# Layer 1's attention scores of seven images as 49 half-width products

## The chip, the cores and the metric

The kernel runs on one core of a Trainium2 chip. The metric is the device time of one execution in microseconds (us). Three runs of the kernel before gave 2888.49, 2889.4 and 2889.59 us; the median is 2889.4 us. PE is the matrix engine, PEld its weight loads, DVE, ACT and POOL are the three elementwise engines, SP only issues transfers. Each engine takes its own list of instructions and meets the others at semaphores.

## The reference

Input x has 8 images of 512 channels and 32 x 32 positions (1024 tokens), all float32. Two attention blocks run one after the other on every image:

```
layer 0:  h = groupnorm(x);  q, k, v = W h + b;  8 heads of 64 channels
          x = x + Wp softmax(q k / 8) v + bp
layer 1:  h = groupnorm(x);  one head of 512 channels
          x = x + Wp softmax((Wq h)(Wk h) / sqrt(512)) (Wv h) + bp
```

In layer 1 the kernel folds weights together: with g = (Wq, Wk product) h the scores are S = h^T g, a 1024 x 1024 matrix contracted over 512 channels, and z = (Wv, Wp product) h replaces the value and the output projection. The change touches how S is made, for seven of the eight images.

## The kernel before

**Products in seven parts.** Nearly every dense product is done by a Strassen-like scheme: both operands are cut in halves along both directions, sums of quarters are formed (`left_sums`, `right_sums`), and seven products p = 1 to 7 of the quarters replace eight. `wino` runs the seven in the order 1, (6, 2, 5, 7) or (2, 5, 6, 7), 4, 3. Partial sums stay in PSUM in three pools of banks called a, b and c with two buffers each. p = 1 goes to bank a and is copied out, 2 is added on top of it in a; 6, 7, 4 accumulate in bank b and are evicted after each; 5 and 3 accumulate in c. The last two steps of each scheme are put on a list, `tail`, and `finish()` emits them after the first step of the next scheme, so that the matrix engine has work while the last sums are evicted.

**Divided twice.** The products with the weights q, k and m (m gives g) are divided twice in `conv2` (L414): each of the seven outer products is itself done as seven inner products j of 128 x 128 x 256. Inner products of two outer products are done together as a `pair`; one pair holds product 7 alone, and there POOL adds finished blocks to each other (`more`, L444). An inner scheme has the steps 1, 6, 2, 5, 7 and, one scheme later, 3 and 4. Step 1 fills bank a and ACT copies it into bank b; 6, 7 and 4 accumulate in b, 2 in a, 5 and 3 in c. So step 7 on PE needs the eviction of step 6 to be over, step 4 that of step 7, and step 3 that of step 5. The quarter sums of the image (`inner_factors`, L411) are made by POOL, four instructions a factor.

**Scores of layer 1.** `layer1_scores` makes g with `conv2` and the list `gsteps` of eight sums of g's quarters. `scores1` (L625) then runs two schemes of the single division, each with 28 products of 128 x 128 x 512. DVE or ACT evicts each block of scores, ACT takes the exponential in place (L645, L648), and DVE sums the exponentials over rows (L654, L656) and forms the eight quarter sums of the exponentials in halves of 512 columns (L170 to L173). `layer1_rest` calls it, then makes z (`by_token`), then the values (`values1`).

**Background work.** Sums that are due later are put on the list `background`, and each step of a scheme takes one to four of them (`run_background`). The row statistics of the next image's group norm (`stats`, L98, L103) run so, inside the scores; its mean and its scale follow inside the scores and inside z as hooks.

**Order.** PE's instructions keep the order of the program. The instructions of DVE, ACT and POOL are put in order when the program is built, unless they are pinned, and each engine then executes its list in that order. One iteration of the loop over images works on layer 0 of image b and layer 1 of image b-1: attention0, projection, g, scores, z, values, then v, k and q of image b+1. Layer 1 of the last image stands alone after the loop and uses a single division for g as well.

## Time and profile before

| what | us |
|---|---|
| median of three runs | 2889.4 |
| time of the profiled execution | 2888.66 |
| its span, first to last instruction | 2886.8 |
| from one image to the next (start of the scores, 493.3 and 846.5) | 353.2 |
| a window of the scores of one image, 493.30 to 541.90 | 48.60 |
| in it: PE, DVE, ACT, POOL busy | 48.60, 31.41, 13.79, 1.04 |

The page lists busy times by engine, the chain of work that ended last and the costliest groups of instructions. Every float32 matmul of the program appears as two records[...], and every weight load likewise; a count "x256" is 128 matmuls. The time between two numbers of a matmul group is not its cost: matmuls overlap, and what counts is the distance from one start to the next.

### The profile page before, as it was taken

Reading aid. Unit: us, or ns where it says so; the run is one execution under the profiler, and the core shown is the slowest. Engines: PE = TensorE matmul, PEld = TensorE weight load, DVE = VectorE, ACT = ScalarE, POOL = GpSimd, SP = SyncE. Lnnn points to the kernel's source line nnn. Section 1 sums busy time; section 2 is a strip of 40 time slices with the busy share of each in tenths; the row PEclk is TensorE's granted clock in tenths of the full one; section 3 lists DMA queues with packets and bytes.
Section 4 is the critical chain, followed back from the end, with each engine's and each line's share of the span. In section 5 each row is a group of like instructions: output and inputs, shape, how many; then the busy total and the mean of one; then the engine's idle time right before and its main releaser. Section 6 shows DMA issues by size and latency. Waiting matters only on the chain.

```text
span 2886.8 us, 30280 instructions
## 1 busy us (share of the span) xinstructions
PE 2871.6 (99%) x11132; PEld 1555.1 (54%) x11132; DVE 2001.5 (69%) x2753; ACT 922.8 (32%) x1201; POOL 704.2 (24%) x781
## 2 busy tenths in 40 slices
PE   9999999999999999999999999999999999999998
PEld 5435635565355653557435574356833558345544
DVE  5587787667876578665786657876588665887554
ACT  1351452215522055211642116421163212632110
POOL 2113224032140321413223222323114131140000
PEclk9999999999999999999999999999999999999999
DMA  8722403123032221322212231122411224021201
GB/s 279 239 96 103 159 19 142 64 105 126 23 135 92 96 107 49 110 92 105 102 48 106 92 136 71 48 106 100 155 49 47 103 106 153 16 81 69 95 0 67
DMA packets 91586, 280.91 MB, mean 97 GB/s; under 512 B 10595, under 2 KB 36387, under 8 KB 82470
## 3 DMA queue, kind: packets, MB, share of 16 engines
q1 hardware_dynamic: 89638, 276.61, 26.4%
q10 hardware_dynamic: 1792, 2.29, 0.3%
q8 instruction: 90, 1.47, 0.2%
q14 instruction: 66, 0.54, 0.1%
HBM read 225.93 MB, written 52.93 MB: 97 GB/s over the span
## 4 chain that ended last, share of the span: by engine, by line
PE 98%; issue 1%; DVE 1%; DMA 0%; POOL 0%; SPq 0%; ACT 0%; DVEq 0%; POOLq 0%
PE sc L67 16%; PE av L67 16%; PE psb_sc L67 6%; PE psb_av L67 6%; PE psa_av L67 4%; PE psa_sc L67 4%; PE psc_av L67 4%; PE psc_sc L67 4%; PE psb_z L67 3%; PE psb_p L67 3%; PE psb_v L67 3%; PE psb_k L67 3%; PE psb_g L67 2%; PE psb_q L67 2%; PE psa_p L67 2%; PE psa_z L67 2%
## 5 line engine op out<-in xcount | busy, mean ns | idle before, releaser
L598 DVE TENSOR_TENSOR sum<-sum,e 128x1024 f32<-128x1024 f32 x384 | 519.3, 1352 | 41.8 <-DVE sum L598 1.4
L594 ACT ACTIVATE e<-sc 128x1024 f32<-128x1024 f32 x512 | 476.8, 1051 | 71.9 <-PE sc L67 71.9
L67 PE MATMUL sc<-q,k 64*128 64x512 f32 x2048 | 458.3, 596 | 0.0
L67 PE MATMUL av<-e,v 128*64 128x512 f32 x2048 | 453.6, 595 | 0.0
L67 PEld LDWEIGHTS sc<-q,k 64*128 64x128 f32 x2048 | 193.2, 186 | 238.4 <-ACT e L594 105.3
L67 PEld LDWEIGHTS av<-e,v 128*64 128x64 f32 x2048 | 141.4, 137 | 304.3 <-issue 302.3
L561 POOL TENSOR_TENSOR all_recs<-all_recs,rc 128x256 f32<-128x256 f32 x72 | 63.6, 884 | 611.2 <-DVE rc L559 603.6
L617 POOL TENSOR_TENSOR a<-a,r 128x512 f32<-128x512 f32 x56 | 114.2, 2039 | 264.4 <-DMA r<-rows 254.8
L559 DVE RECIPROCAL rc<-sums 128x256 f32<-128x256 f32 x72 | 126.5, 1757 | 47.7 <-PE sums L67 26.9
L612 ACT COPY a<-av 128x512 f32<-128x512 f32 x64 | 37.5, 586 | 305.4 <-PE av L67 305.4
L596 DVE TENSOR_TENSOR sum<-e,e 128x1024 f32<-128x1024 f32 x64 | 78.7, 1230 | 59.0 <-ACT e L594 58.9
L67 PE MATMUL psa_sc<-g,h 128*128 128x512 f32 x256 | 115.2, 595 | 0.0
L648 ACT ACTIVATE e<-e 128x512 f32<-128x512 f32 x96 | 59.7, 629 | 168.5 <-DVE e L647 168.5
L67 PE MATMUL psa_av<-e,z 128*128 128x512 f32 x256 | 113.3, 595 | 0.0
L128 POOL TENSOR_TENSOR rstd<-ve,mhalf 128x4 f32<-128x4 f32 x16 | 36.2, 2263 | 260.9 <-DVE ve L126 260.9
L140 ACT ACTIVATE h<-h,b,s 128x1024 f32<-128x1024 f32 x62 | 78.5, 1267 | 58.4 <-DMA h<-in_x 45.9
L411 POOL TENSOR_TENSOR inner_h<-h,inner_h 128x256 f32<-128x256 f32 x112 | 96.0, 860 | 2.7
L411 POOL TENSOR_TENSOR inner_h<-h 128x256 f32<-128x256 f32 x56 | 57.2, 1022 | 151.3 <-PE psc_av L67 151.3
L444 POOL TENSOR_TENSOR k<-k,k 128x256 f32<-128x256 f32 x28 | 20.1, 728 | 299.9 <-DVE u_k L439 299.9
L67 PEld LDWEIGHTS psa_sc<-g,h 128*128 128x128 f32 x256 | 48.1, 190 | 60.2 <-issue 54.5
L67 PEld LDWEIGHTS psa_av<-e,z 128*128 128x128 f32 x256 | 48.0, 190 | 57.3 <-issue 55.7
L652 POOL COPY sum<-e 128x1024 f32<-128x1024 f32 x8 | 8.8, 1102 | 283.5 <-ACT e L648 283.5
(327 smaller groups left out, 4992.1 us busy)
## 6 DMA issues: line engine op xcount, KB each, us to landing
x<-in_x SPq DMA_DIRECT2D x36, 512.0 KB
h<-in_x SPq DMA_DIRECT2D x32, 512.0 KB
spill<-x SPq DMA_DIRECT2D x32, 512.0 KB
h<-spill SPq DMA_DIRECT2D x32, 512.0 KB
x<-spill SPq DMA_DIRECT2D x32, 512.0 KB
out<-x SPq DMA_DIRECT2D x64, 256.0 KB
w_p<-sums_p SPq DMA_DIRECT2D x8, 1792.0 KB
r<-rows SPq DMA_DIRECT2D x112, 128.0 KB
```

The lines of the kernel that those rows point to most:

```text
L67: tc.keep_in_program_order(nc.tensor.matmul(*args, **kw))
L128: nc.gpsimd.tensor_tensor(rstd, ve, mhalf, ALU.pow)
L140: tc.keep_in_program_order(nc.scalar.activation(dst, src, AF.Identity, bias=b, scale=s))
L411: pin(nc.gpsimd.tensor_tensor(dst, x, y, ALU.subtract))
L559: nc.vector.reciprocal(rc, sums)
L561: nc.gpsimd.tensor_tensor(all_recs, all_recs, rc, ALU.add)
L594: nc.scalar.activation(e, sc, AF.Exp, scale=(C // 8) ** -0.5)
L596: nc.vector.tensor_add(total, es[0], e)
L598: nc.vector.tensor_add(total, total, e)
L612: nc.scalar.copy(dst, av)
L617: nc.gpsimd.tensor_tensor(dst, dst, r, ALU.mult)
L648: nc.scalar.activation(dst, dst, AF.Exp, scale=scale)
```

## The change

`scores1` stays for the last image only. The other seven use the new `scores1_twice`: each of the seven outer products p of the scores is divided again into seven inner products, 49 products with a width of 256, and each is two matmuls of 128 x 128 x 256. The inner scheme of `conv2` is taken out into `inner_steps`, which both use. POOL forms the inner factors of g (`query_factors`, four instructions for each p), at the start of the scheme before the one that uses them. The outer products come in the order 1, 2, 5, 6, 7, 3, 4. For outer products 1 and 5 ACT evicts four of the inner steps; elsewhere DVE adds each eviction to a block that is already there. For product 7 POOL adds blocks to each other, eight times, each 128 x 512. Exponentials are taken over tiles of 128 x 1024, row sums and quarter sums of the exponentials likewise; four of the eight quarter sums go to POOL. The last steps of g are now emitted after the first step of the scores. Four of the twelve statistics run inside g, the other eight in the scores; the hooks for mean and scale both move into z.

```
-                def step(j):
...
+        def inner_steps(uid, parity, k, mm, add, y, x, extra, after7, final, early=()):
+            def put(dst, n, at):
+                if x is None:
+                    (d,) = dst
+                    nc.scalar.copy(d, ps[n])
+                else:
+                    add(dst, ps[n], x(*at))
+            def step(j):
+                if j == 1:
+                    bank("a")
+                    mm(ps["a"], 1, True)
+                    bank("b")
+                    nc.scalar.copy(ps["b"], ps["a"])
...
+                elif j == 7:
+                    mm(ps["b"], 7, False)
+                    add(y(1, 1), ps["b"], [tmp["c5"]])
+                    extra(1, 1, False, True)
...
+                elif j == 4:
+                    mm(ps["b"], 4, False)
+                    put(y(1, 0), "b", (1, 0))
+                    extra(1, 0, True, True)
+                run_background(1)
+            step(1)
+            finish()
+            for g in early:
+                g()
+            for j in (6, 2, 5, 7):
+                step(j)
+            for g in after7:
+                g()
+            tail.extend([lambda: step(3), lambda: step(4)])
+            tail.extend(final)
...
+        def query_factors(f, uid):
+            t = big_tile(f"inner_{uid}", (P, 4, 2 * P))
...
+            for dst, x, y, op in (
+                (s1, a21, a22, ALU.add), (s2, s1, a11, ALU.subtract), (s3, a11, a21, ALU.subtract),
+                (s4, a12, s2, ALU.subtract),
+            ):
+                tc.keep_in_program_order(nc.gpsimd.tensor_tensor(dst, x, y, op))
...
+        def scores1_twice(b, f, gf, gsteps, first, uid, stats):
...
+            def add(dst, ps, x):
+                nc.vector.tensor_add(dst[0], ps, x[0])
+            def more(dst, x, y, r, cc):
+                nc.gpsimd.tensor_tensor(blocks(dst, r, cc)[0], blocks(x, r, cc)[0], blocks(y, r, cc)[0], ALU.add)
+            def exps(r, c):
+                for cc in (1, 0):
+                    nc.scalar.activation(e[c, cc, r], e[c, cc, r], AF.Exp, scale=scale)
+            def add_up(r, c):
+                if r == c:
+                    return [lambda: nc.vector.tensor_add(parts[r], e[c, 0, r], e[c, 1, r])]
+                return [
+                    *(lambda cc=cc: nc.vector.tensor_add(parts[r], parts[r], e[c, cc, r]) for cc in range(2)),
+                    lambda: nc.gpsimd.tensor_tensor(total[:, r, :], parts[r][:, 0, :], parts[r][:, 1, :], ALU.add),
+                ]
+            def product(s, p, y, x, before, small, after7=(), final=()):
+                def mm(ps, j, start):
+                    for i in range(2):
+                        matmul(
+                            ps[:, i, :], f[p][j][:, ts(i, P)], g2[p][j], start=start and i == 0, stop=True, skip_group_check=True
+                        )
+                def extra(r, cc, read, written):
+                    if p == 7:
+                        if read:
+                            more((0, 1), (0, 1), (1, 1), r, cc)
+                        if written:
+                            more((1, 1), (1, 0), (1, 1), r, cc)
...
+            product(0, 1, (1, 0), None, [2], gsteps[:2] + stats[:5])
+            product(1, 2, (0, 0), (1, 0), [5], gsteps[2:4], (), [lambda: exps(0, 0)])
+            product(2, 5, (1, 1), None, [6, 4], gsteps[4:] + stats[5:])
+            product(3, 6, (0, 1), (1, 0), [7, 3], add_up(0, 0))
+            product(4, 7, (1, 0), (0, 1), [], [])
+            product(5, 3, (0, 1), (0, 1), [], [], [lambda: exps(1, 1)], [lambda: exps(0, 1)])
+            product(
+                6, 4, (1, 0), (1, 0), [], add_up(1, 1) + add_up(0, 1), (),
+                [lambda: exps(1, 0), lambda: background.extend(add_up(1, 0) + steps)],
+            )
...
+            engines = [nc.vector] * 4 + [nc.gpsimd] * 4
...
-                gf = layer1_scores(b - 1, hf, inner)
+                gf, gsteps = layer1_scores(b - 1, hf, inner, [[], [lambda: background.extend(stats[:4])]])
+                _, _, mean, affine = norm_hooks(norm1, f"1_{b}")
...
-                hooks = [[], [], [lambda: background.extend(stats)]], [[], [], *means], affine
-                layer1_rest(b - 1, hf, gf, hooks, ahead)
+                layer1_rest(b - 1, hf, inner, gf, gsteps, stats[4:], [[], mean, [], affine], ahead)
```

## The prediction

> **What bounds the kernel now.** I read the shares by engine, then the chain, the groups by shape, single durations, and the time line around one image.

> ```profile
> PE 2871.6 (99%) x11132; PEld 1555.1 (54%) x11132; DVE 2001.5 (69%) x2753; ACT 922.8 (32%) x1201; POOL 704.2 (24%) x781
> PE 98%; issue 1%; DVE 1%; DMA 0%; POOL 0%; SPq 0%; ACT 0%; DVEq 0%; POOLq 0%
> ...
> 493.30:541.90 48.60, 48.60 (x124) 23.03 (x123) 31.41 (x56) 13.79 (x23) 1.04 (x1) 1.00 0.10 38
> ```

> PE holds 98% of the chain, and in the window of one image's scores (last line: length, then busy time of PE, PEld, DVE, ACT, POOL) it never rests. So a shorter PE list is worth its full length, and every new wait of PE costs its full length.

> ```profile
> L67 PE MATMUL psa_sc<-g,h 128*128 128x512 f32 x256 | 115.2, 595 | 0.0
> L67 PE MATMUL psb_g<-inner_h,w_m 128*128 128x256 f32 x294 | 75.1, 383 | 0.3
> ...
> 479.18 0.59 PE L67 MATMUL psa_g<-h,w_m 128*128 128x256 f32 x2
> 479.61 0.59 PE L67 MATMUL psa_g<-t_h,w_m 128*128 128x256 f32 x2
> ...
> 491.46 0.30 PEld L67 LDWEIGHTS psc_g<-h,w_m 128*128 128x128 f32 x2 [0.46 <-DVE c_g L439]
> ```

> The means 595 and 383 ns overlap. The starts say more: a pair of 256-wide records (one matmul) starts every 0.43 us, so 0.2165 a record; eight 512-wide ones run from 457.68 to 461.11, 0.429 each. The last line is g's stage, divided twice: PE waits for a DVE eviction there.

> ```profile
> L444 POOL TENSOR_TENSOR g<-g,g x28: 724/729/737, 485.4 to 2608.8; 128x256 f32<-128x256 f32 x28
> L617 POOL TENSOR_TENSOR a<-a,r x56: 1274/2156/2365, 150.8 to 2559.5; 128x512 f32<-128x512 f32 x56
> L306 POOL TENSOR_TENSOR prepare_q<-prepare_q 128x896 f32<-128x896 f32 x4 | 8.3, 2088 | 25.4 <-DMA x<-in_x 25.3
> L647 DVE TENSOR_TENSOR e<-psc_sc,u_sc 128x512 f32<-128x512 f32 x32 | 22.0, 686 | 8.4 <-PE psc_sc L67 8.4
> L654 DVE TENSOR_TENSOR sum<-sum,e 128x1024 f32<-128x1024 f32 x24 | 29.3, 1219 | 5.6 <-ACT e L648 5.6
> L856 DVE TENSOR_TENSOR x<-x,t_p x16: 673/1122/1246, 283.2 to 2589.4; 128x512 f32<-128x512 f32 x16
> L594 ACT ACTIVATE e<-sc 128x1024 f32<-128x1024 f32 x512 | 476.8, 1051 | 71.9 <-PE sc L67 71.9
> ```

> These are the prices: POOL adds (minimum, median, maximum where there are three), a DVE eviction, DVE sums, an exponential.

> [...] g's POOL adds keep to 724 to 737 ns beside DVE's evictions from PSUM, while L856, SBUF to SBUF beside POOL, has a median of 1122 ns and a minimum of 673. [...]

> **The change part by part, per image.** The instruction lists of the two built programs give the order on each engine, and no times. They are alike for all seven images.

> 1. PE's products. Before: 56 matmuls, 112 records x 0.429 = 48.05, and 0.28 of small waits inside (sum of the starts that come late). After: 98 matmuls, 196 x 0.2165 = 42.43. Gain 5.9 us, 41 us over seven images. A step is now two matmuls, 0.87 us, and the eviction of a step has one other step's time between (bank b: 7 after 6, 4 after 7; bank c: 3 after 5). An eviction starts 1.1 us after its step begins and takes 0.69; the next use comes at 2.6. So DVE may be 0.8 us late and no more.

> 2. Statistics in g: four of 0.67 us stand between g's evictions, the last just behind the first eviction of the pair that holds one product, where a step lasts 0.43. PE's step 7 there comes at 486.6 in place of 485.4, and one wait (491.46) goes away since the scores' first step lies between: +0.9.

> 3. Start of the scores (+1.0, from 0.6 to 1.45). ACT has the last four bias additions of g (0.72, later 0.65) before the copies of outer product 1; they wait for g's last evictions at about 495.2. Its eviction of step 5 ends near 499.9, PE's step 3 is due at 499.3. DVE's first two sums of g wait for the same bias, with POOL making factors beside them, so 0.65 to 1.1 each, and step 4 behind them is late.

> 4. Outer product 2 (+1.4, from 1.2 to 1.6). DVE: six evictions, 4.15, four sums of g, 2.6 to 4.4, and statistics left over, 1.7, in a scheme of 6.06 us of PE. The lists put a sum between evictions each time.

> 5. Outer products 5 and 6 (+0.4, from 0 to 0.85): row sums of 1.22, up to 2.1 beside POOL, ahead of evictions.

> 6. Outer product 7, then 3. POOL adds eight blocks of 128 x 512. From 256 (0.727) and 896 (2.083) elements a line gives 1.27; twice 0.727 bounds it at 1.45. DVE only evicts from PSUM then, so no contention. Count from U, the start of this scheme's step 6. The first add follows the eviction at U + 1.85, the chain of eight ends at U + 12.2 (POOL has finished its factors about 3 us before U), that is V + 6.1, where V = U + 6.06 is step 6 of outer product 3. PE itself does not need these. But the exponentials of the last blocks do: ACT takes the second at V + 6.2 to 7.3. **DVE's list has the row sum of exactly these exponentials ahead of the eviction of step 7**, although the program writes it a product later. So DVE waits to V + 7.3, sums to 8.55, evicts to 9.25; PE's step 4, due at V + 5.2, accumulates in that bank and starts at 9.3. Cost +4.2, with restart; to 5.3 if the adds take 1.45.

> 7. Free edits. Outer product 4 and z: DVE has 6.9 us of work in a scheme of 6.06, but z's first step (3.46 us of PE) follows; without that cover 0.9. The first POOL factors start as g's adds end (491.3 before, about 492.8 now), and are first needed at 495; POOL's later factors are a whole product ahead. ACT has about 17 us of work in 42. Quarter sums of the exponentials: POOL's four, 2.4 to 3.8 each, end well inside the values' 48 us. Mean and scale move later in z; rstd (2.26) and three small ones now queue behind two POOL subtractions, so the scale is ready near 567 where it was 555.9; ACT needs it at 575.4, since the image's load lands then. Without those 8 us it would delay the next image. SP has 512 rows in both programs; its loads after the scores wait for buffers that the scores have left by then.

> Sum: -5.9 + 0.9 + 1.0 + 1.4 + 0.4 + 4.2 = +2.0; a restarted PE loses about another 0.1 at each of several waits (104 ns late on the second record after 491.46), so +2.2. Times seven: +15 us. The profiled execution's 2888.66 becomes 2904; the median stands 0.7 above it, so 2905. All low ends together, -5.9 + 6.7 = +0.8, give 2895; all high ones, -5.9 + 10.9 = +5, give 2924.

> **The rivals.** (A) DVE's early row sum does not hold: the POOL chain ends before the eviction would start. For it: POOL is 76% idle in the profile. Against: eight adds need 10 us and the scheme has 6. Then -5.9 + 3.7 + 0.3 = -1.9, 2876. (B) The early waits (2 to 5) hide in one another, since a late PE gives DVE time, and only 6 stays: -5.9 + 4.3 = -1.6, 2878: faster. For it: the gaps of g's stage are small, 0.7 us an image. Against: g has no such sums in its schemes. All waits hidden would be 2848; the sign turns where the waits sum to 5.9. (C) POOL's adds meet contention and take 2.04 us as L617's mean does: the chain ends 6 us later, +8.2 an image, 2947. Against: L444's narrow spread. That PE's products do not shrink is excluded: g's stage shows their rate.

> **How the numbers follow.** The main case 0.72 (own range 2895 to 2924), B 0.12, A 0.06, C 0.04, a sum near zero 0.06. About 0.2% (5.8 us) is what a measurement can tell from none. Faster: A, B and a little, 0.19. Same: the middle and the low edge of the main case, 0.09. Slower 0.72. The range for 8 in 10 reaches down into B, to 2880, and up to 2924; A, the rest of B, C and the tails are left out.

> **What would show it.** Late starts of PE in outer product 3, at the last step 4 of bank b, of 4 to 5 us in each of seven images, with DVE idle ahead of a 128x1024 row sum, released by ACT, whose exponential was released by POOL. POOL's 128x512 adds at 1.27 to 1.45 us. Scores with 196 records at 0.2165 and, g's end to z's start, about 50.5 us in place of 48.6. PE waits of 0.5 to 1.5 us in outer products 1 and 2. Wrong if the POOL adds run near 0.7, if DVE's exponential is ready by V + 4, or if z or the values show new waits.

## The result and the profile after

The changed kernel takes 2906.48 us (median of five runs, 2902.85 to 2908.49) against 2888.85 us before (median of five runs, 2888.40 to 2889.59): a ratio of 1.006, with a 95% interval of 1.0045 to 1.0075. That is 17.6 us more. The forecast was 2905, slower, with a range from 2880 to 2924. The profiled execution took 2908.49 us, its span is 2906.6 (before: 2886.8).

The page of the changed kernel, shares by engine and then the chain that ended last:

```profile
PE 2852.4 (98%) x11720; PEld 1678.3 (58%) x11720; DVE 2098.9 (72%) x2760; ACT 953.8 (33%) x1222; POOL 1018.8 (35%) x1068
...
PE 90%; DVE 4%; POOL 3%; issue 1%; ACT 1%; DMA 0%; SPq 0%; DVEq 0%; POOLq 0%; ACTq 0%
```

PE has 588 records more, 84 an image, as counted. It is less busy, 2852.4 us for 2871.6. But its share of the chain has fallen from 98% to 90%; DVE and POOL have most of the difference. The window of one image's scores (length, then busy time and count of PE, PEld, DVE, ACT, POOL, then the granted clock of the matrix engine, DMA share, GB/s):

```profile
493.10:542.80 49.70, 45.28 (x198) 38.22 (x197) 35.15 (x56) 17.69 (x26) 33.34 (x37) 0.97 0.10 38
```

PE rests for 4.4 of 49.7 us, where it never rested. The mean clock that it was granted is 0.97 (1 is full speed), where it was 1.00; nothing in the prediction answers to that.

The waits of PE, from the view that lists them by the engine and line that ended them (us in total, times, longest):

```profile
PE psb L67 <- DVE e L712: 29.8, 21, 3.7
PE psb_g L67 <- DVE u_g L521: 6.3, 7, 0.9
PE psb_av L67 <- DVE w_av L238: 1.9, 4, 0.5
```

Seven of the 21 waits in the first line are the long one, 7 x 3.7 = 26 of 29.8 us. Two groups of the page's list by line answer to the prices, POOL's additions and the first row sum:

```profile
L715 POOL TENSOR_TENSOR e<-e,e 128x512 f32<-128x512 f32 x56 | 69.9, 1268 | 21.3 <-DVE u L712 19.7
L724 DVE TENSOR_TENSOR sum<-e,e 128x1024 f32<-128x1024 f32 x14 | 17.1, 1221 | 25.5 <-ACT e L719 25.5
```

POOL's additions take 1268 ns, 1.27 as worked out. The row sum L724 has 25.5 us of idle DVE time ahead of it, seven times 3.6, all ended by ACT's exponential. Here is that place in the first of the seven images, from the time lines of POOL, ACT, DVE and PE (start, length, what, idle time before and what ended it):

```profile
523.54 10.21 POOL L715 TENSOR_TENSOR e<-e,e 128x512 f32<-128x512 f32 x8 [2.80 <-DVE u L712]
...
533.79 1.06 ACT L719 ACTIVATE e<-e 128x1024 f32<-128x1024 f32 x1 [1.51 <-POOL e L715]
...
534.88 1.23 DVE L724 TENSOR_TENSOR sum<-e,e 128x1024 f32<-128x1024 f32 x1 [3.63 <-ACT e L719]
536.02 0.68 DVE L712 TENSOR_TENSOR e<-psb,c 128x512 f32<-128x512 f32 x1
...
532.01 1.03 PE L67 MATMUL psc<-inner,h 128*128 128x256 f32 x4
536.76 2.08 PE L67 MATMUL psb<-sg,inner_h 128*128 128x256 f32 x4 [3.72 <-DVE e L712]
538.62 1.76 PE L67 MATMUL psb<-inner,inner_h 128*128 128x256 f32 x4
540.23 1.03 PE L67 MATMUL psa<-g,t_h 128*128 128x256 f32 x4
```

Read from top to bottom this is the chain of the prediction: eight additions, exponential, row sum, the eviction of step 7 behind it, and only then PE's step 4. With V = 527.70 (step 6 of outer product 3) POOL ends at V + 6.05 (said: 6.1), the exponential at V + 7.15 (7.3), the eviction at V + 9.0 (9.25), and PE starts at V + 9.06 (9.3).

The last two lines hold what was not foreseen. From 538.62 to 540.23 four records take 1.61 us from start to start, where four took 0.86 before the wait. The window view splits that stretch (PE's busy time and count come after the length; the granted clock is the third number from the end):

```profile
532.80:536.70 3.90, 0.24 (x2) 0.00 (x0) 1.82 (x3) 1.54 (x2) 0.95 (x1) 1.00 0.00 0
536.70:540.10 3.40, 3.34 (x8) 2.72 (x9) 1.29 (x3) 1.56 (x2) 0.00 (x0) 0.50 0.00 0
540.10:543.50 3.40, 3.40 (x18) 3.00 (x17) 2.90 (x4) 0.55 (x1) 0.00 (x0) 1.00 0.02 5
```

PE is idle for most of 3.9 us; then come 3.4 us at a granted clock of 0.50, the half rate, with 8 records; then 1.00 and 18 records in the same time. In five images this costs 1.74 us (the sum of the starts that come late after the wait). In the two others it costs 3.04: there the granted clock stays at half for 6.83 us, and PE works through some 6.0 of them.

### The profile page after: what moved, and what is told of

It is laid out like the page before. It is cut to its first block, busy times and chain, and to the rows that moved or that the text cites. A ratio compares the mean times of both kernels' runs of the same rounds, so it can differ in the third digit from the quotient of the medians.

```text
span 2906.6 us, 32039 instructions
## 1 busy us (share of the span) xinstructions
PE 2852.4 (98%) x11720; PEld 1678.3 (58%) x11720; DVE 2098.9 (72%) x2760; ACT 953.8 (33%) x1222; POOL 1018.8 (35%) x1068
## 4 chain that ended last, share of the span: by engine, by line
PE 90%; DVE 4%; POOL 3%; issue 1%; ACT 1%; DMA 0%; SPq 0%; DVEq 0%; POOLq 0%; ACTq 0%
PE sc L67 16%; PE av L67 15%; PE psb_av L67 5%; PE psa_av L67 4%; PE psc_av L67 4%; PE psb L67 4%; PE psb_z L67 3%; PE psb_p L67 3%; PE psb_v L67 3%; PE psb_k L67 3%; PE psb_g L67 2%; PE psb_q L67 2%; POOL e L715 2%; PE psa_p L67 2%; PE psa_z L67 2%; PE psc_v L67 2%
## 5 line engine op out<-in xcount | busy, mean ns | idle before, releaser
L617 DVE TENSOR_TENSOR sum<-sum,e 128x1024 f32<-128x1024 f32 x384 | 519.3, 1352 | 41.8 <-DVE sum L617 1.8
L613 ACT ACTIVATE e<-sc 128x1024 f32<-128x1024 f32 x512 | 476.8, 1053 | 72.2 <-PE sc L67 72.2
L67 PE MATMUL sc<-q,k 64*128 64x512 f32 x2048 | 458.4, 597 | 0.0
L67 PE MATMUL av<-e,v 128*64 128x512 f32 x2048 | 453.6, 596 | 0.0
L67 PEld LDWEIGHTS sc<-q,k 64*128 64x128 f32 x2048 | 193.5, 186 | 238.1 <-ACT e L613 105.2
L67 PEld LDWEIGHTS av<-e,v 128*64 128x64 f32 x2048 | 141.4, 137 | 304.3 <-issue 302.3
L67 PE MATMUL psa_av<-e,z 128*128 128x512 f32 x256 | 113.3, 596 | 0.0
L67 PE MATMUL psb<-inner,inner_h 128*128 128x256 f32 x392 | 106.5, 397 | 0.0
L140 ACT ACTIVATE h<-h,b,s 128x1024 f32<-128x1024 f32 x62 | 78.3, 1268 | 80.4 <-DMA h<-in_x 64.9
L411 POOL TENSOR_TENSOR inner_h<-t_h 128x256 f32<-128x256 f32 x84 | 85.0, 1015 | 17.9 <-PE psc_av L67 15.4
L67 PEld LDWEIGHTS psb<-inner,inner_h 128*128 128x128 f32 x392 | 78.2, 200 | 11.5
L719 ACT ACTIVATE e<-e 128x1024 f32<-128x1024 f32 x56 | 58.4, 1055 | 77.4 <-POOL e L715 42.0
L67 PE MATMUL psb_g<-inner_h,w_m 128*128 128x256 f32 x294 | 75.2, 384 | 6.3 <-DVE u_g L521 6.3
L67 PEld LDWEIGHTS psa_av<-e,z 128*128 128x128 f32 x256 | 48.1, 190 | 57.2 <-issue 56.5
L715 POOL TENSOR_TENSOR e<-e,e 128x512 f32<-128x512 f32 x56 | 69.9, 1268 | 21.3 <-DVE u L712 19.7
```

The source lines that it names most:

```text
L67: tc.keep_in_program_order(nc.tensor.matmul(*args, **kw))
L140: tc.keep_in_program_order(nc.scalar.activation(dst, src, AF.Identity, bias=b, scale=s))
L411: pin(nc.gpsimd.tensor_tensor(dst, x, y, ALU.subtract))
L613: nc.scalar.activation(e, sc, AF.Exp, scale=(C // 8) ** -0.5)
L617: nc.vector.tensor_add(total, total, e)
L715: nc.gpsimd.tensor_tensor(blocks(dst, r, cc)[0], blocks(x, r, cc)[0], blocks(y, r, cc)[0], ALU.add)
```

## Experiments

Two questions stand behind the 17.6 us. Is it the place of one row sum in DVE's list that makes the wait, or is POOL's chain too long wherever the sum stands? And what is the half rate? Each run was measured beside the kernel before on the same chip, which took 2888.2 to 2888.4 us there; the changed kernel's 2906.5 is from the result above, where before took 0.4 to 0.6 us more.

### The row sum moved behind the evictions

```
-                nc.vector.tensor_add(dst[0], ps, x[0])
+                tc.keep_in_program_order(nc.vector.tensor_add(dst[0], ps, x[0]))
...
-                    return [lambda: nc.vector.tensor_add(parts[r], e[c, 0, r], e[c, 1, r])]
+                    return [lambda: tc.keep_in_program_order(nc.vector.tensor_add(parts[r], e[c, 0, r], e[c, 1, r]))]
```

> The changed kernel with one difference: VectorE takes the additions of the scores and the row sum of the second diagonal quarter in the order written, so that this sum stands behind the three evictions of outer product 3 and the first of outer product 4. All work is kept. Theory (the sum's place in VectorE's list makes the wait): the wait of 3.9 us at step 4 of outer product 3 goes, and with it the time after it in which matmuls start 0.42 us apart instead of 0.216 (about 2 us per image). But ScalarE's copy for outer product 4 stands behind the two exponentials that wait for GpSimd's additions, and would end some 1.5 to 1.9 us after step 6 of outer product 4 is due. If a wait that short brings no half rate: 3.9 + 2.2 - 1.7 = 4.4 us saved per image, 2906.5 - 7 x 4.4 = 2876 us (2870 to 2884). If it brings the half rate as well: 2906.5 - 7 x 2.2 = 2891 us. Rival (GpSimd's chain is late for TensorE by any way, and its wait only changes its place): within 5 us of 2906.

Measured: 2875.4 us (2875.17 to 2876.2), ratio to before 0.9954 (0.9937 to 0.9971). The sign of the whole change has turned, with the same work, by the order of DVE's list alone. The edit moves two row sums an image, each behind four evictions; the sum of the first diagonal quarter moves too, but no matmul waited behind that one in the changed kernel. The wait has gone from outer product 3, and the shorter one foretold for outer product 4 is there, in PE's time line:

```profile
531.64 1.03 PE L67 MATMUL psb<-sg,inner_h 128*128 128x256 f32 x4
534.17 1.13 PE L67 MATMUL psb<-inner,inner_h 128*128 128x256 f32 x4 [1.50 <-ACT psb L459]
```

The second row starts 1.66 us late, behind ACT's copy. The window after it:

```profile
534.20:537.60 3.40, 3.40 (x16) 3.01 (x17) 2.19 (x3) 1.84 (x2) 0.00 (x0) 1.00 0.02 5
```

The clock stays at 1.00, and in all seven images no matmul after the wait is slow. The rival (POOL's chain binds by any way) is refuted as far as the sum goes: POOL's eight additions take what they took (1269 ns on the mean, 1268 before the edit).

### The exponentials behind the copy as well

```
-            product(5, 3, (0, 1), (0, 1), [], [], [lambda: exps(1, 1)], [lambda: exps(0, 1)])
+            product(5, 3, (0, 1), (0, 1), [], [], (), [lambda: exps(1, 1), lambda: exps(0, 1)])
```

and, so that ACT keeps to it:

```
-                    nc.scalar.copy(ps["b"], ps["a"])
+                    tc.keep_in_program_order(nc.scalar.copy(ps["b"], ps["a"]))
...
-                    nc.scalar.activation(e[c, cc, r], e[c, cc, r], AF.Exp, scale=scale)
+                    tc.keep_in_program_order(nc.scalar.activation(e[c, cc, r], e[c, cc, r], AF.Exp, scale=scale))
```

> As the run before, and the two exponentials of the second diagonal quarter stand on ScalarE behind the copy that begins outer product 4. All work is kept. Theory: nothing that waits for GpSimd's additions stands ahead of an eviction or a copy any more, so both the wait and the half rate after it go: 3.9 + 2.2 = 6.1 us per image, 2906.5 - 7 x 6.1 = 2864 us (2859 to 2870), 25 us below the kernel before. Rival (the lateness is handed on to the sums and exponentials of the last quarter and from there to the reciprocals or to GpSimd's part of the normalization): a new wait of 1 to 3 us per image at outer product 4 or in z, 2871 to 2885 us.

Measured: 2864.88 us (2864.66 to 2865.6), ratio to before 0.9917 (0.9901 to 0.9934), 24 us below the kernel before and 42 below the change as made. No new wait took the place of the two. The waits of PE by this kernel's list:

```profile
PE psb_g L67 <- DVE u_g L521: 6.3, 7, 0.9
...
PE psb L67 <- DVE e L712: 3.7, 14, 0.3
```

The 29.8 us of the changed kernel have become 3.7. So the cause of the wait is settled: a sum and two exponentials that nothing was in a hurry for, ahead of an eviction and a copy that PE was waiting for.

### The idle time filled

This kernel adds work: eight matmuls an image into a tile that nothing reads, where PE would stand idle. Theory C is that the half rate is an answer to PE's idle time.

```
                 elif j == 4:
+                    fill()
                     mm(ps["b"], 4, False)
...
+            def fill():
+                ps = acc_tile(f"fill_{uid}")
+                for n in range(8):
+                    matmul(ps[:, : 2 * P], f[3][1][:, :P], g2[3][1], start=True, stop=True)
...
+                    fill if p == 3 else lambda: None,
```

> The changed kernel with eight additional 128x256 matmuls per image (3.5 us at the rate of the profile, into a PSUM tile that nothing reads) on TensorE just ahead of step 4 of outer product 3, where TensorE otherwise stands idle for 3.9 us. The wait itself, its cause and all other work are as in the changed kernel. Theory C [...]: the granted clock stays at 1 there, matmuls after the wait start 0.216 us apart, and 1.7 to 3.3 us per image are saved: 2906.5 - 7 x 2.2 = 2891 us (2883 to 2895). Rival D (the half rate comes from what runs beside those matmuls: the row sum, the exponentials, late evictions): it stays, and the time is 2906 us or a few us more.

Measured: 2892.04 us (2889.38 to 2893.42): 14.4 us less than the changed kernel, with 3.5 us more work an image and the same wait for the same eviction. Windows of the idle stretch, now filled, and of what follows:

```profile
531.20:534.90 3.70, 3.70 (x18) 2.92 (x16) 1.59 (x2) 1.54 (x2) 0.99 (x1) 1.00 0.00 0
535.00:538.40 3.40, 3.21 (x15) 2.85 (x16) 2.43 (x5) 2.11 (x2) 0.00 (x0) 1.00 0.02 5
```

The row sum, the exponentials and the late evictions run beside these matmuls as before, and the clock is 1.00 in all seven images. The half rate is an answer to the idle time. This run also shows the change with its wait and without the half rate: 2892.0 us against 2888.4 before, a ratio of 1.001.

Half as many matmuls leave a part of the idle time:

```
-                for n in range(8):
+                for n in range(4):
```

> As the run before with four additional matmuls instead of eight (1.7 us), so that some 2.2 us of idle time are left at the same place. [...] Theory C [...]: part of the half rate stays, between the time with eight and 2906. Rival D: 2906 us.

Measured, with four matmuls: 2899.7 us (2895.56 to 2902.99). This lies between, as Theory C had it if any idle time counts; the author's other guess, no half rate after so short a rest and a time within 2 us of the kernel with eight, is missed. PE's start is 2.16 us late in every image (2.00 us of rest in the trace), and the half rate follows in four of the seven, at 1.68 us each; the last section shows what sets these four apart. One image without and one with, the idle stretch of the first and what comes behind the wait in each:

```profile
533.40:535.40 2.00, 0.11 (x1) 0.00 (x0) 1.77 (x3) 0.68 (x2) 0.00 (x0) 1.00 0.00 0
535.40:538.80 3.40, 3.29 (x15) 2.93 (x16) 2.43 (x5) 2.11 (x2) 0.00 (x0) 1.00 0.00 0
...
890.30:892.30 2.00, 2.00 (x7) 1.55 (x6) 0.69 (x1) 0.95 (x2) 0.00 (x0) 0.50 0.00 0
```

### Undoing parts: the statistics

```
-                gf, gsteps = layer1_scores(b - 1, hf, inner, [[], [lambda: background.extend(stats[:4])]])
+                gf, gsteps = layer1_scores(b - 1, hf, inner, [[], [lambda: background.extend(stats[:0])]])
...
-            product(2, 5, (1, 1), None, [6, 4], gsteps[4:] + stats[5:])
+            product(2, 5, (1, 1), None, [6, 4], gsteps[4:] + stats[5:9])
...
-            product(4, 7, (1, 0), (0, 1), [], [])
+            product(4, 7, (1, 0), (0, 1), [], stats[9:])
...
-                layer1_rest(b - 1, hf, inner, gf, gsteps, stats[4:], [[], mean, [], affine], ahead)
+                layer1_rest(b - 1, hf, inner, gf, gsteps, stats, [[], mean, [], affine], ahead)
```

> The changed kernel with one part undone: the first four steps of the statistics, which the change moved into g, stand in the scores again (nine of the twelve in outer products 1 and 5 and their tails, the last three in outer product 7). All work is kept. Theory: the wait of 1.06 us that the trace of the changed kernel has in g, 0.53 us per image above the kernel before, goes, and outer products 1 and 2 wait as before: 2906.5 - 7 x 0.53 = 2902.8 us. Rival (the additions of VectorE are late by the sum of its work at the start of the scores, so that statistics moved there cost as much as in g): 2906.5 us, plus or minus 1.

Measured: 2911.96 us (2909.12 to 2914.65), worse than the theory and than its rival. By the late starts of PE in the first image the wait in g does go (1.26 to 0.41 us). But outer products 1 and 2 now cost 2.33 in place of 1.64, and outer product 6 has a new wait of 1.02, because a statistics step and the row sum stand together ahead of an eviction: 0.69 + 1.02 - 0.85 = +0.86, times seven 6.0, which is what the time shows (5.5). Of these two places g was the cheaper one for the four statistics.

To take them out of the dense parts altogether, the kernel of 2864.88 us was given four steps each behind the evictions of outer products 6, 7 and 3:

```
-            product(0, 1, (1, 0), None, [2], gsteps[:2] + stats[:5])
+            product(0, 1, (1, 0), None, [2], gsteps[:2])
...
-            product(2, 5, (1, 1), None, [6, 4], gsteps[4:] + stats[5:])
-            product(3, 6, (0, 1), (1, 0), [7, 3], add_up(0, 0))
-            product(4, 7, (1, 0), (0, 1), [], [])
+            product(2, 5, (1, 1), None, [6, 4], gsteps[4:])
+            product(3, 6, (0, 1), (1, 0), [7, 3], add_up(0, 0) + stats[:4])
+            product(4, 7, (1, 0), (0, 1), [], stats[4:8])
...
```

The last four follow in outer product 3 (`stats[8:]` in its call), and none are left in g.

> The run with the sum and the exponentials behind (2864.9 us), and the statistics moved out of g and out of outer products 1 and 2: four steps each in the background of outer products 6, 7 and 3, where VectorE has 0.2 to 1 us free between its evictions. All work is kept. Theory: g's wait (0.53 us above before) goes, and of the waits at the starts of outer products 1 and 2 (1.6 us per image) the part that statistics ahead of an eviction make, 0.4 to 0.8 us: 2864.9 - 7 x (0.53 + 0.6) = 2857 us (2853 to 2861). Rival (an eviction of outer products 6, 7 or 3 is late behind a statistics step of 0.6 us, and TensorE waits there instead): 2861 to 2868 us.

Measured: 2895.22 us (2889.8 to 2902.46), 30 us worse than without the move, far outside both. DVE's time line at outer product 6:

```profile
515.90 1.64 DVE L724 TENSOR_TENSOR sum<-e,e 128x1024 f32<-128x1024 f32 x1
518.76 0.69 DVE L712 TENSOR_TENSOR e<-psa,e 128x512 f32<-128x512 f32 x1 [1.22 <-PE psa L67]
```

The eviction at 518.76 reads a bank that PE had finished near 516, and yet it waited for PE. In the built program it waits for step 1 of outer product 7 (517.62 to 518.65 in PE's time line), which reads g's first tile: the statistics hold x's tiles longer, and the tile of the exponentials that this eviction writes first came into the buffer of that g tile. PE's steps 3 and 4 were late by 2.3 and 1.1 us, with the half rate after it in three images. One buffer more tests this:

```
-NBIG = 32
+NBIG = 33
```

> The run with the statistics moved to outer products 6, 7 and 3 (2895.2 us), with 33 instead of 32 buffers in the pool of 4 KB tiles. All work is kept. In the trace of that run the first addition of outer product 6 into the exponentials' tile starts 1.2 us after the row sum ahead of it has ended, when step 1 of outer product 7 has ended on TensorE, and TensorE's steps 3 and 4 of outer product 6 are late by 2.3 and 1.2 us, in three images at half rate after that. Theory B (the statistics hold their inputs' buffers longer, so that this tile comes into the buffer of g's first tile, which step 1 of outer product 7 still reads): with one buffer more the tile comes into another, the wait goes, and what remains is the run with sum and exponentials behind, less 0.85 us in g and plus 0.1 to 0.6 us at the start of the scores: 2860 us (2857 to 2864). Rival (the statistics steps of 0.6 us ahead of the evictions of outer product 6 are the cause): 2885 to 2896 us.

Measured: 2866.06 us (2862.64 to 2868.01), ratio to before 0.9923 (0.9909 to 0.9937). The buffer was the cause of the 29 us, and the rival, that the statistics steps themselves make the wait, is refuted: they stand where they stood. What the move was meant to gain is not there, so that the forecast of 2860 (2857 to 2864) is missed by a little: g is 0.85 us an image shorter, but PE's step 4 of outer product 1 starts 1.0 us late in place of 0.48 (a sum of g has moved ahead of the eviction that it needs), and outer product 6 has 0.9 us of new waits. It is equal to the kernel of 2864.88 within what can be told.

### Undoing parts: the quarter sums, and the wait in the values

The changed kernel's trace has a wait in the values in four of seven images, with the time lines of DVE and PE:

```profile
602.48 7.51 DVE L783 TENSOR_TENSOR o<-o,r 128x512 f32<-128x512 f32 x1
...
611.78 1.55 PE L67 MATMUL psb_av<-t,z 128*128 128x512 f32 x3 [0.47 <-DVE w_av L238]
```

The same multiplication has a median of 692 ns. It reads two tiles in SBUF, and POOL runs a closed row of additions of 0.72 us from SBUF for the next image meanwhile. The kernel before has such a row in the values too, and its longest multiplication takes 1.24 us. The first question is whether POOL's four quarter sums, which the change put ahead of that row, make the difference:

```
-            engines = [nc.vector] * 4 + [nc.gpsimd] * 4
+            engines = [nc.vector] * 8
```

> The changed kernel with one part undone: all eight sums of the exponentials' quarters in z are VectorE's, instead of four on VectorE and four on GpSimd. All work is kept. In the trace of the changed kernel the values hold a wait of 0.73 us in four of the seven images, beside a VectorE multiplication of 7.5 us (0.69 elsewhere), while GpSimd forms factors of the next image. Theory V (GpSimd's four sums of z push its work on the factors into the multiplications of the values): no such wait in any image, 2906.5 - 4 x 0.73 = 2903.6 us, unless VectorE's four more sums of 1.2 us delay the evictions of z. Rival W (the wait hangs on the phase of the two engines' streams in the values, which these sums don't set): it stays in some images, 2904 to 2908 us. In the run with filled idle time it came in one image of seven and in the run with the sum behind in none, with the sums where the change put them, which speaks for W.

Measured: 2923.84 us (2923.16 to 2924.83). The wait in question is left in one image, where a multiplication takes 8.0 us and PE's start behind it is 1.14 us late; so it does not need POOL's four sums, as rival W had it. But a larger wait, 2.2 us in six images and 1.7 in the last, stands at the start of the values and makes the time. DVE's and PE's time lines:

```profile
583.99 0.69 DVE L780 TENSOR_TENSOR o<-psa_av,r 128x512 f32<-128x512 f32 x1 [1.90 <-PE psa_av L67]
584.60 0.68 DVE L159 TENSOR_TENSOR sz<-z,z 128x512 f32<-128x512 f32 x1
...
585.43 1.95 PE L67 MATMUL psc_av<-t,sz 128*128 128x512 f32 x4 [1.48 <-DVE sz L159]
```

It is not the four sums themselves: DVE sits idle for 1.90 us. With the other list the order changed, and the scaling of the first blocks, which waits for PE, stands ahead of z's sums, for which PE waits. That is the row sum's case again. As the order changed with the edit, the run does not say why four images became one.

A direct test delays POOL's row of additions, in the kernel of 2866.06 us: a copy of one column of x on POOL stands ahead of them, and they are pinned behind it.

```
+                tc.keep_in_program_order(nc.gpsimd.tensor_copy(g, done_x[0][:, :1]))
             background.extend(steps)
```

> The run before, and GpSimd's 28 additions for the factors of the next image's h (0.72 us each, back to back through the middle of the values) start only when VectorE has made the last additions of the values: a copy of one column of x on GpSimd stands ahead of them and waits for it. All other work is kept. Theory W (VectorE's multiplication of two SBUF operands takes 7.5 us, and TensorE then waits 0.63 + 0.1 us, where it meets this stream): no image has the wait of 0.73 us in the values, against four of seven in the changed kernel and two to four in others; 0 to 3 us less than the run before. Rival (the stream is not the cause): the wait stays in some images. Against both: the factors may be late for k, 17 us later, which would cost 1 us or more per image there.

Measured: 2867.64 us (2866.27 to 2868.12), no such wait in any image; but the run before, without the copy, had none either in its trace, so this says nothing. The copy let the row start at 602.1, in the midst of the values and not after them. The same edit in the changed kernel, where four images had the wait:

> The changed kernel itself with the one edit of the run before: GpSimd's additions for the factors of the next image's h wait, by a copy of one column of x on GpSimd, until VectorE has made one of the later additions of the values (602 us in the trace of the run before, where the stream otherwise begins near 583). All other work is kept. Theory W (VectorE's multiplications of two SBUF operands stand still for 7.5 us where they meet GpSimd's stream): the multiplications behind the gate still meet it, those ahead of it do not, so that the wait of 0.73 us comes in fewer images than four, most likely in none: 2903 to 2907 us. Rival (the wait has another cause): four images again, 2906.5 us. The difference in time is at most 3 us; the trace decides, by the number of multiplications of 7.5 us.

Measured: 2902.97 us (2901.65 to 2904.72), 3.5 us less than the changed kernel. No multiplication is longer than 1.14 us and no image has the wait. Part of the 3.5 us is the half rate: this trace has none in one image and two windows of it in one, where the changed kernel's trace has two windows in two. So the time decides nothing here, but the trace does: the edit touches POOL's list alone, and DVE's keeps the order of the changed kernel.

That POOL's row is what the multiplication waits for shows in its end as well. The traces of this document hold eighteen multiplications of 7.5 to 8.0 us, and each of them ends 0.47 us after the start of the last addition of POOL's row; PE was late behind every one. Seventeen of the eighteen start 0.07 to 0.12 us before POOL's next addition. Of eighteen others that start so, fifteen took 0.69 to 0.71 us, and there POOL's next addition took 1.15 to 1.19 us in place of 0.72; three took some 1.35 us. So either engine can be the one that gives way. Which one, and so why it is none to four of seven images in kernels that differ elsewhere, stays open.

## Why the prediction was right, and where it was not

The time and the sign were met, 2905 said and 2906.5 measured, and the wait that the prediction rests on was right in place, chain and size. That the number was met all the same is luck: the balance behind it, in us per image from the starts of PE's records that come late, has wrong terms that made up for each other.

| step | said | measured |
|---|---|---|
| 1 products | -5.9 | -6.0 |
| 2 statistics in g | +0.9 | +0.53 |
| 3 start of the scores | +1.0 | +0.98 |
| 4 outer product 2 | +1.4 | +0.66 |
| 5 outer products 5 and 6 | +0.4 | 0 |
| 6 wait behind the row sum | +4.2 | +3.88 |
| restarts | +0.2 | in the terms |
| half rate after the wait | - | +1.74 in five images, +3.04 in two: 2.11 |
| 7 "free edits": z, values | 0 | +0.08; 0.42 (0.74 in four of seven) |
| sum | +2.2 | +2.7 |

2.66 x 7 = 18.6, against 19.8 between the spans; where the rest is was not traced. Steps 1 to 6 alone, at their measured sizes, sum to +0.05 us an image, which is no change. What makes the kernel slower is the half rate behind the wait, 2.11, and the wait in the values, 0.42; the prediction had about 0.1 for a restart and nothing in their place. The run with the idle time filled says the same with 2892.0 us, where the half rate is missing.

**Step 1** was right: 196 records of 0.216 us, 42.3 us. The 0.28 us of waits inside the old scores are part of the 6.0.

**Step 2** was too large. PE's step 7 in g came 0.85 us later than before, not 1.2; the wait that should go did go (0.32).

**Step 3** was right in place and size: the first late start stands behind ACT's copy, which waits behind the bias additions (0.33), the second behind DVE's two sums and a statistics step (0.47).

**Steps 4 and 5** were too large. Here DVE's sums of g took 0.68 to 0.90 us beside POOL, near the low end of the range of 0.65 to 1.1 that was taken, and the start that was late already gave DVE time. Outer products 5 and 6 had none. So rival B was right in part: steps 2 to 5 cost 2.2 us and not 3.7. With the 3.88 of step 6 that just cancels the gain of step 1, so that B's sign, faster, does not come out either.

**Step 6** was right to 0.3 us in each of its members, and the runs show its cause: with the sum moved, the sign turns. That DVE takes its list in order, on which the case rests, shows in the same lines: PE's step 7 for the late eviction ran from 530.28 to 531.31, DVE was free from 531.25 on, and yet the eviction started at 536.02, behind the sum. A and C are refuted by the lines of the result (DVE idle 3.63 us; additions of 1.27). The prediction looked at the order of DVE's list, which the program's text doesn't give.

**The term that failed** is "a restarted PE loses about another 0.1". That was read from waits of 0.5 us. After 3.9 us PE loses 2.11 us on the mean. The trace of the kernel before does not show such a loss: after PE's first matmul its longest rest is 0.80 us, and from 9.2 us of the span to the last matmul the granted clock is 1.00. So the 0.1 was carried from waits of 0.5 us to one of 4.2. With the measured 2.11 in place of the 0.2 for restarts the sum would have been +4.1, 2918 us, a worse forecast from a better reason, since steps 2, 4 and 5 were 1.5 us too large together.

**Step 7** had one miss, and it is one of the prediction's own signs of being wrong: the values show a new wait. The step looked at where POOL's work ends, and not at POOL's factors for the next image, which run beside the multiplications of the values. What L856 shows in the trace before, an addition of two SBUF tiles that took 1.12 to 1.25 us beside POOL's additions and 0.67 where POOL was idle, was used for row sums and the sums of g, and not for this multiplication, which has two SBUF operands beside a POOL row; 7.51 us for 0.69 (8.02 in one run) is what it comes to here. The rest of the step held: the row sums, z and the scale hid as said, but for 0.08 us.

**The range.** The ends of the prediction's sum, +0.8 and +5, do not follow from the ranges that its steps give; with the restarts those make about +1.2 and +4.4. The measured time lies inside either way.

## What to carry to other kernels

Before a shorter list of the bottleneck engine is worth anything, look in the built order of every other engine for an instruction that waits for a slow neighbour and stands ahead of one that the bottleneck needs; four of the ten runs here turned on such a place, and putting two row sums an image behind four evictions each was worth more than the change cost (31 us to 17.6). Price a wait of the matrix engine of 2 us or more with the half rate that may follow: a rest of 2.00 us had it in four of seven images, and the one of 3.72 in all seven, where it cost 2.11 us an image, 14.8 of the 17.6. And a moved reader moves buffers: look at what each first write into a pool's tile waits for.

## What the hardware showed that was not expected

```profile
530.38:533.79 3.41, 1.59 (x8) 1.06 (x6) 0.00 (x0) 1.90 (x3) 2.23 (x2) 1.00 0.00 0
533.79:537.21 3.42, 1.52 (x7) 1.37 (x8) 2.78 (x4) 1.42 (x2) 0.00 (x0) 1.00 0.00 0
537.21:540.62 3.41, 3.41 (x18) 3.00 (x17) 3.06 (x5) 1.17 (x2) 0.00 (x0) 1.00 0.02 5
...
2289.57:2292.98 3.41, 1.43 (x7) 0.93 (x5) 2.19 (x5) 0.57 (x1) 2.99 (x4) 1.00 0.00 0
2292.98:2296.39 3.41, 2.47 (x10) 1.92 (x11) 2.73 (x6) 0.00 (x0) 0.00 (x0) 1.00 0.00 0
...
886.08:889.49 3.41, 1.41 (x7) 0.93 (x6) 2.08 (x3) 1.54 (x2) 0.20 (x1) 1.00 0.00 0
889.49:892.90 3.41, 3.41 (x9) 2.69 (x9) 1.03 (x2) 1.99 (x2) 0.00 (x0) 0.50 0.00 0
```

In the first three lines the usual rest of 3.72 us falls across two windows, PE is idle for 1.82 and 1.90 us of them, and the clock stays at 1.00: the one image of seven without the half rate. In the next pair PE is busy for 1.43 us of the first window, and the clock of the second stays full; in the last pair it is busy for 1.41, and the second has half. Over the twelve traces, all 34 windows within the program with 1.995 us or more of idle PE were followed by the half rate, and none of the nearly ten thousand others at full clock, which have 1.974 at most. A half-rate window with up to 0.55 us of idle PE was the last one; with 0.63 or more another followed, which makes the two double ones of the changed kernel (0.87 and 0.74). This is what sets four of seven images apart in the run with four matmuls: the same rest of 2.00 us lies within one window in four, and is split in three (1.88 and 0.11 the most uneven). An estimate from these figures: a rest of PE under 1.98 us cannot bring the half rate, one above twice that, 3.96, cannot miss it, and between them it is a matter of where the windows fall; 3.72 us had it in 27 of 28 images.

A DVE multiplication of two SBUF operands took 7.5 to 8.0 us in place of 0.69 beside an unbroken row of POOL additions of 0.72 us in eighteen cases of these traces, and ended in each 0.47 us after the start of the row's last addition.
